# Group statistics by one sum and one sum of squares, bias on GpSimd, and a loop on TensorE, in a normalize-and-convolve kernel

## The chip, the cores and the metric

The kernel runs on one core of a Trainium2 chip. The metric is the device time of one execution in microseconds (us), the median of several runs. A core has TensorE (PE; PEld is its weight load), VectorE (DVE), ScalarE (ACT), GpSimd (POOL) and SyncE (SP), which run side by side and wait for each other by semaphores, and 16 DMA engines that move data between the memory of the chip (HBM) and the on-chip buffer SBUF. TensorE writes to PSUM.

## The reference

For 8 images of 32 channels and 128 x 128 points, fp32:

```python
def _gn(v, G=16, eps=1e-5):            # groups of 2 channels
    g = v.reshape(B_, G, C_ // G, H_, W_)
    m = jnp.mean(g, axis=(2, 3, 4), keepdims=True)
    s = jnp.var(g, axis=(2, 3, 4), keepdims=True)
    return ((g - m) / jnp.sqrt(s + eps)).reshape(v.shape)

# _L0_conv_ref: zero-padded to 256 x 256, fft2 of x and of the 3x3 weights (norm="ortho"),
# product summed over input channels, ifft2, real part, and then a window of it:
    sh = (fft_H - out_h) // 2          # 64
    out = sp[:, :, sh:sh + out_h, sw:sw + out_w]
    return out + bias[None, :, None, None]

x = x + _L0_conv_ref(_gn(x), weight, bias, 1, 1)
```

The window starts 64 rows and columns into the padded result. So the convolution reaches only one corner of the output (66 x 66 points, 33 x 33 of each parity), scaled by 1/256; everywhere else the output is x plus the bias. The statistics still need every point of x.

## The kernel before

The host lays x out so that a partition holds one of the four (row, column) parities of a channel: 4 x 32 = 128 partitions of 64 x 64 points for an image, two images to a pair. The loads are cut as below and are all issued at once on SyncE:

```python
for img in range(2):                       # images 0 and 1: two halves each
    for half in range(2):
        load(xts[img][:, rows, :], x[0, :, img, rows, :])
        if img == 0 and half == 0:
            weights_in = load(wb_sb, wb)
for img in range(2):                       # images 2 and 3: one load each
    loaded[2 + img] = [(H, load(xts[2 + img], x[1, :, img]))]
for pair in range(2, NPAIR):               # images 4 to 7: one load a pair
    loaded[2 * pair] = loaded[2 * pair + 1] = [(H, load(pairs[pair], x[pair]))]
```

Every instruction is recorded by a helper, `put(engine, emit, *needs)`, that gives it the waits it needs. The steps of an image:

```python
def take_stats(img):                       # VectorE: 8 x BN_STATS of 512 elements
    for s in range(NSTAT):
        put("dve", lambda e: e.bn_stats(stats[img][:, s, :], ...), *rows_in(...))
def aggregate(img):                        # VectorE aggregate; ScalarE: the terms to be averaged
    mv_ok = put("dve", lambda e: e.bn_aggr(mv, ...))
    put("act", lambda e: e.activation(t[:, 0:NSIGN], signs, AF.Identity, scale=mv[:, 0:1]), mv_ok, bias_ok)
    put("act", lambda e: e.activation(t[:, NSIGN:], mv[:, 1:2], AF.Identity, bias=eps, scale=float(FFT * FFT)))
def group(img):                            # TensorE: average over the 8 partitions of a group
    put("pe", lambda e: e.matmul(ps_ms[:, 0 : NSIGN + 1], avg, terms[img], start=True, stop=True), ...)
def normalize(img):
    square_ok = put("act", ... activation(squares, ps_ms[:, 1:NSIGN], AF.Square, accum_out=var[:, 0:1]) ...)
    copied = put("dve", ... tensor_copy(var[:, 1:2], ps_ms[:, NSIGN : NSIGN + 1]) ...)
    std_ok = put("act", ... activation(std, var[:, 0:1], AF.Sqrt, bias=var[:, 1:2]) ...)
    rstd_ok = put("dve", ... reciprocal(rstd[:, 0:1], std) ...)
    shift_ok = put("act", ... activation(rstd[:, 1:2], ps_ms[:, 0:1], AF.Identity, scale=rstd[:, 0:1]) ...)
    for rows in (slice(0, ROWS + 1), slice(ROWS + 1, N)):        # g in two pieces, 12 and 21 rows
        normal[img].append(put("act", lambda e: e.activation(g[:, rows, :], xt[...], AF.Identity,
                           bias=rstd[:, 1:2], scale=rstd[:, 0:1]), shift_ok, ...))
def add_bias(img):                         # ScalarE: x + bias where the convolution doesn't reach
    for part in (low, right):              # 1984 and 1023 elements a partition
        put("act", lambda e: e.activation(part, part, AF.Identity, bias=bias_sb), *free)
def multiply(img, n):                      # TensorE: 4 matmuls for a third of the image
    for k in range(4):
        put("pe", lambda e: e.matmul(ps[...], w_sb[:, k * P : (k + 1) * P], g[...],
            start=(k == 0), stop=(k == 3)), w_ok, normal[img][min(n, 1)], ...)
def add(img, first, last):                 # VectorE: x + convolution + bias
    put("dve", lambda e: e.scalar_tensor_tensor(part, in0=ps, scalar=bias_sb, in1=part, ...), *conv_ok[img], bias_ok)
```

An fp32 matmul shows in the profile as two matmuls and two weight loads. The order:

```python
keep_warm(H // 2, 2); take_stats(0); aggregate(0); group(0); warm_ok = keep_warm(0, 1)
normalize(0); add_bias(0); take_stats(1)
for img in range(B):
    more = img + 1 < B
    multiply(img, 0); multiply(img, 1)
    if more: aggregate(img + 1)
    if img:
        add(img - 1, 0, NCHUNK)
        ...                                # stores: pairs 0 and 1 whole, then images 4, 5, 6
    if more:
        group(img + 1); normalize(img + 1); add_bias(img + 1)
    multiply(img, 2)
    if img + 2 < B: take_stats(img + 2)
store(low rows of image 7); add(7, 0, 2); add(7, 2, NCHUNK); store(the rest of image 7)
```

Before that, VectorE builds `avg` (ones over 8 within a group, else zero) from what GpSimd has made, and ScalarE spreads bias, signs and weights to the four parities in 20 small copies (`spread`). TensorE's instructions are written out, all 107 matmuls.

Of the kernel before, what the change touches and what calls it, by code (L numbers as in the profile page):

```python
# [30 lines left out]
STATS = 8  # L32
BANK = 512
NSIGN = 8
# [3 lines left out]
class Queues:  # L38
# [5 lines left out]
    def __init__(self, nc):  # L44
        self.nc = nc
        self.names = {"pe": nc.tensor, "dve": nc.vector, "act": nc.scalar, "pool": nc.gpsimd, "sp": nc.sync}
        self.sems = {}
        self.done = {}
        self.seen = {name: {} for name in self.names}
        for name in self.names:  # L50
            if name != "sp":
                self.sems[name] = nc.alloc_semaphore(f"done_{name}")
                self.done[name] = 0
# [9 lines left out]
    def __call__(self, name, emit, *needs, mark=False, adds=None):  # L63

        engine, seen = self.names[name], self.seen[name]
        waits = {}
        for token, of in needs:
            if seen.get(of, 0) < token[of]:
                waits[of] = max(waits.get(of, 0), token[of])
        for token, of in needs:  # L70
            self._learn(name, token)
        waits = list(waits.items())
        for of, value in waits[:-1]:
            engine.wait_ge(self.sems[of], value)
        op = emit(engine)
        if waits:
            of, value = waits[-1]
            op.wait_op(self.sems[of], value, "sem-ge")
        if adds is not None:
            of, by = adds, LANDED  # L80
        elif mark:
            of, by = name, 1
        else:
            return None
        op.then_inc(self.sems[of], by)
        self.done[of] += by
        return {**seen, of: self.done[of]}, of


def conv_preact_kernel(nc: bass.Bass, x: bass.AP, wb: bass.AP, out: bass.AP):  # L90
# [7 lines left out]
    NSTAT = H // STATS  # L98
# [9 lines left out]

    pairs = [sbuf(f"x{pair}", P, 2, H, W) for pair in range(NPAIR)]
    xts = [pairs[img // 2][:, img % 2] for img in range(B)]  # L110
    wb_sb = sbuf("wb_sb", C, 9 * C + 4 * (1 + NSIGN))
# [7 lines left out]
    for img in range(2):  # L119
        loaded[img] = []  # L120
        for half in range(2):
            rows = slice(half * H // 2, (half + 1) * H // 2)
            loaded[img].append((rows.stop, load(xts[img][:, rows, :], x[0, :, img, rows, :])))
            if img == 0 and half == 0:
                weights_in = load(wb_sb, wb)
# [9 lines left out]

    pair = sbuf("pair", P, P // 2, 2)
# [4 lines left out]
    pair_ok = put("pool", lambda e: e.memset(pair, 0.125), mark=True)  # L141
    for step, base in ((-1, 0), (1, 1)):
# [8 lines left out]
    w_zero = put("pool", lambda e: e.memset(w_sb, 0.0), mark=True)  # L151
    eps_ok = put("dve", lambda e: e.memset(eps, EPS * FFT * FFT), mark=True)
    pair2 = pair.rearrange("p a b -> p (a b)")
    sums = put(
        "dve", lambda e: e.tensor_add(avg[:, 0 : 2 * C], pair2[:, 0 : 2 * C], pair2[:, 2 * C : 4 * C]),
# [3 lines left out]
        "dve", lambda e: e.tensor_add(avg[:, 2 * C : 3 * C], avg[:, 0:C], avg[:, C : 2 * C]), sums, mark=True  # L159
    )  # L160
    for k in (0, 1, 3):
        avg_ok = put(
            "dve", lambda e: e.tensor_copy(avg[:, k * C : (k + 1) * C], avg[:, 2 * C : 3 * C]), sums, mark=True
        )

    put("act", lambda e: e.activation(warm, eps, AF.Sqrt), eps_ok)  # L166

    bs_sb = sbuf("bs_sb", P, 1 + NSIGN)  # L170
    bias_sb, signs = bs_sb[:, 0:1], bs_sb[:, 1:]
    taps = wb_sb[:, 0 : 9 * C].rearrange("p (a b o) -> p a b o", a=3, b=3)
    w6 = w_sb.rearrange("p (dr dc r q o) -> p dr dc r q o", dr=2, dc=2, r=2, q=2)
    places = {

        0: ((0, slice(0, 1), slice(2, 3)), (1, slice(0, 2), slice(0, 2))),
        1: ((0, slice(0, 2), slice(1, 3)), (1, slice(1, 2), slice(0, 1))),
    }

    def spread(to, of):  # L180
        return put("act", lambda e: e.activation(to, of, AF.Identity), weights_in, w_zero, mark=True)  # L181

    for q in range(4):
        rin, cin = q // 2, q % 2
        to = slice(q * C, (q + 1) * C)
        of = 9 * C + q * (1 + NSIGN)
        bias_ok = spread(bs_sb[to, :], wb_sb[:, of : of + 1 + NSIGN])
        for dr, r, a in places[rin]:
            for dc, c, b in places[cin]:
                w_ok = spread(w6[to, dr, dc, r, c, :], taps[:, a, b, :])  # L190

    gs = [sbuf(f"g{k}", P, N, N) for k in range(2)]
    stats = [sbuf(f"stats{img}", P, NSTAT, 6) for img in range(B)]
    mvs = [sbuf(f"mv{k}", P, 2) for k in range(B)]
    terms = [sbuf(f"terms{k}", P, NSIGN + 1) for k in range(B)]
    squares = [sbuf(f"square{k}", P, NSIGN - 1) for k in range(B)]
    variances = [sbuf(f"var{k}", P, 2) for k in range(B)]
    stds = [sbuf(f"std{k}", P, 1) for k in range(B)]
    rstds = [sbuf(f"rstd{k}", P, 2) for k in range(B)]
# [3 lines left out]
    stats_ok, terms_ok, group_ok, means_read, normal, conv_ok, biased, added = {}, {}, {}, {}, {}, {}, {}, {}  # L203
    warm_ok = None

    def take_stats(img):
        for s in range(NSTAT):
            stats_ok[img] = put(
                "dve",
                lambda e: e.bn_stats(  # L210
                    stats[img][:, s, :],
                    xts[img][:, STATS * s : STATS * (s + 1), :].rearrange("p h w -> p (h w)"),
                ),
                *rows_in(img, STATS * (s + 1)), mark=s == NSTAT - 1,
            )

    def aggregate(img):

        mv, t = mvs[img], terms[img]
        mv_ok = put(  # L220
            "dve", lambda e: e.bn_aggr(mv, stats[img].rearrange("p n s -> p (n s)")), stats_ok[img], mark=True  # L221
        )
        put("act", lambda e: e.activation(t[:, 0:NSIGN], signs, AF.Identity, scale=mv[:, 0:1]), mv_ok, bias_ok)  # L223
        terms_ok[img] = put(
            "act",
            lambda e: e.activation(t[:, NSIGN:], mv[:, 1:2], AF.Identity, bias=eps, scale=float(FFT * FFT)),  # L226
            mark=True,
        )

    def group(img):  # L230

        group_ok[img] = put(
            "pe",
            lambda e: e.matmul(ps_ms[:, 0 : NSIGN + 1], avg, terms[img], start=True, stop=True),  # L234
            terms_ok[img], avg_ok, *means_read.get(img - 1, ()), mark=True,
        )

    def normalize(img):
        xt, g, var, std, rstd = xts[img], gs[img % 2], variances[img], stds[img], rstds[img]

        square_ok = put(
            "act",
            lambda e: e.activation(squares[img], ps_ms[:, 1:NSIGN], AF.Square, accum_out=var[:, 0:1]),  # L243
            group_ok[img], mark=True,
        )
        copied = put(

            "dve", lambda e: e.tensor_copy(var[:, 1:2], ps_ms[:, NSIGN : NSIGN + 1]), square_ok, mark=True  # L248
        )

        std_ok = put(
            "act", lambda e: e.activation(std, var[:, 0:1], AF.Sqrt, bias=var[:, 1:2]), square_ok, copied, mark=True  # L252
        )
        rstd_ok = put("dve", lambda e: e.reciprocal(rstd[:, 0:1], std), std_ok, mark=True)  # L254
        shift_ok = put(
            "act",
            lambda e: e.activation(rstd[:, 1:2], ps_ms[:, 0:1], AF.Identity, scale=rstd[:, 0:1]),  # L257
            rstd_ok, mark=True,
        )
        means_read[img] = (copied, shift_ok)  # L260
        normal[img] = []
        for rows in (slice(0, ROWS + 1), slice(ROWS + 1, N)):
# [7 lines left out]
                    shift_ok, *rows_in(img, H), *conv_ok.get(img - 2, ()), mark=True,  # L270
# [3 lines left out]
    def add_bias(img):  # L274
# [4 lines left out]
        free = [*normal[img]] + ([warm_ok] if img == 0 else [])  # L279
        biased[img] = [  # L280
            put("act", lambda e: e.activation(part, part, AF.Identity, bias=bias_sb), *free, mark=True)  # L281
# [3 lines left out]
    def multiply(img, n):  # L285
# [3 lines left out]
        for k in range(4):  # L289
# [4 lines left out]
            needs = [w_ok, normal[img][min(n, 1)]] + added.get(img - 2, [])  # L294
            ok = put(
                "pe",
                lambda e: e.matmul(  # L297
# [28 lines left out]
    def keep_warm(first, times):  # L326
        piece = xts[0][:, first : first + STATS, :].rearrange("p h w -> p (h w)")
        for _ in range(times):
            ok = put(
                "pe", lambda e: e.matmul(ps_w, avg, piece, start=True, stop=True),  # L330
                avg_ok, *rows_in(0, H), mark=True,
# [3 lines left out]
    keep_warm(H // 2, 2)  # L335
    take_stats(0)
    aggregate(0)
    group(0)
    warm_ok = keep_warm(0, 1)
    normalize(0)  # L340
    add_bias(0)
    take_stats(1)
    for img in range(B):
        more = img + 1 < B
        multiply(img, 0)
        multiply(img, 1)
        if more:
            aggregate(img + 1)
        if img:
# [3 lines left out]
            elif img > 4:  # L353
                store(out[(img - 1) // 2, :, (img - 1) % 2], xts[img - 1], *finished(img - 1))
        if more:
            group(img + 1)
            normalize(img + 1)
            add_bias(img + 1)
        multiply(img, 2)
        if img + 2 < B:  # L360
            take_stats(img + 2)
# [60 lines left out]
```

## Time and profile before

| | |
|---|---|
| median of 3 runs | 84.51 us (84.22 to 84.69) |
| span of the profiled execution | 82.9 us |
| instructions in the profile | 697 |
| busy: PE, DVE, ACT, POOL | 65.0, 54.5, 52.0, 2.3 us |
| moved by DMA | 33.63 MB, mean 405 GB/s |

The profile is of one execution. Times in it are counted from the start of the span. A group of instructions is given by its line in the kernel, engine, operation, output<-input, shape, count, busy time in us and mean ns of one, and then the idle time of the engine before it. Names are the program's own without buffer numbers: `ps` is the result of the convolution, `ps_m` the averaged statistics, `g` the normalized corner. The 16 completion marks of a transfer, one from each DMA engine, and the single packets are also in the trace.

### The profile page before, as it was taken

Reading aid. Unit: us, or ns where it says so; the run is one execution under the profiler, and the core shown is the slowest. Engines: PE = TensorE matmul, PEld = TensorE weight load, DVE = VectorE, ACT = ScalarE, POOL = GpSimd, SP = SyncE. Lnnn points to the kernel's source line nnn. Section 1 sums busy time; section 2 is a strip of 40 time slices with the busy share of each in tenths; the row PEclk is TensorE's granted clock in tenths of the full one; section 3 lists DMA queues with packets and bytes.
Section 4 is the critical chain, followed back from the end, with each engine's and each line's share of the span. In section 5 each row is a group of like instructions: output and inputs, shape, how many; then the busy total and the mean of one; then the engine's idle time right before and its main releaser. Section 6 shows DMA issues by size and latency. Waiting matters only on the chain.

```text
span 82.9 us, 697 instructions
## 1 busy us (share of the span) xinstructions
PE 65.0 (78%) x214; PEld 39.4 (47%) x214; DVE 54.5 (66%) x103; ACT 52.0 (63%) x102; POOL 2.3 (3%) x8
## 2 busy tenths in 40 slices
PE   0000999999999999999999999999999999950000
PEld 0000431666666656666666665666566566610000
DVE  0329946991999699799969988996998160042000
ACT  6109527995996699489759948984995797000000
POOL 6400000000000000000000000000000000000000
PEclk9999999999999999999999999999999999998555
DMA  2899999999996997999889998998999999999991
GB/s 40 332 411 431 407 442 478 387 427 450 514 490 269 506 490 324 427 506 474 292 364 442 442 490 348 427 506 379 427 387 427 435 411 466 403 442 400 417 430 82
DMA packets 2211, 33.63 MB, mean 405 GB/s; under 512 B 256, under 2 KB 288, under 8 KB 416
## 3 DMA queue, kind: packets, MB, share of 16 engines
q1 hardware_dynamic: 2208, 33.60, 96.1%
q8 instruction: 1, 0.02, 0.1%
q14 instruction: 2, 0.02, 0.1%
HBM read 16.82 MB, written 16.78 MB: 405 GB/s over the span
## 4 chain that ended last, share of the span: by engine, by line
PE 76%; DMA 8%; DVE 2%; ACT 2%; SPq 1%; issue 1%
PE ps L297 70%; DMA x<-x_dram 8%; PE ps_w L330 5%; DVE x L312 2%; PE ps_m L234 1%; SPq L117 1%; ACT g L266 1%; ACT std L252 0%; ACT square L243 0%; ACT rstd L257 0%; DVE rstd L254 0%; DVE var L248 0%
## 5 line engine op out<-in xcount | busy, mean ns | idle before, releaser
L297 PE MATMUL ps<-g,w_sb 128*128 128x363 f32 (+1 forms) x192 | 59.0, 464 | 0.2 <-ACT g L266 0.2
L297 PEld LDWEIGHTS ps<-g,w_sb 128*128 128x128 f32 x192 | 35.2, 189 | 21.6 <-ACT g L266 2.0
L210 DVE BATCH_NORM_STATS2 stats<-x 128x6 f32<-128x512 f32 x64 | 38.7, 678 | 2.5 <-DMA x<-x_dram 2.4
L281 ACT ACTIVATE x<-x,bs_sb 128x1984 f32<-128x1984 f32 (+1 forms) x16 | 23.9, 1543 | 0.3
L312 DVE SCALAR_TENSOR_TENSOR x<-ps,bs_sb,x 128x1089 f32<-128x1089 f32 (+2 forms) x9 | 10.5, 1179 | 7.2 <-PE ps L297 7.2
L266 ACT ACTIVATE g<-x,rstd 128x396 f32<-128x396 f32 (+1 forms) x16 | 12.7, 840 | 0.3
L330 PE MATMUL ps_w<-x,avg 128*128 128x512 f32 x6 | 5.8, 1111 | 8.4 <-DMA x<-x_dram 8.4
L330 PEld LDWEIGHTS ps_w<-x,avg 128*128 128x128 f32 x6 | 1.7, 328 | 9.4 <-DMA x<-x_dram 8.4
L243 ACT ACTIVATE square<-ps_m 128x7 f32<-128x7 f32 x8 | 1.4, 178 | 5.7 <-PE ps_m L234 5.7
L248 DVE COPY var<-ps_m 128x1 f32<-128x1 f32 x8 | 1.3, 158 | 5.1 <-ACT square L243 5.1
L223 ACT ACTIVATE terms<-bs_sb,mv 128x8 f32<-128x8 f32 x8 | 2.4, 303 | 3.5 <-DVE mv L221 3.5
L234 PEld LDWEIGHTS ps_m<-terms,avg 128*128 128x128 f32 x16 | 3.2, 205 | 2.8 <-ACT terms L226 1.3
L252 ACT ACTIVATE std<-var 128x1 f32<-128x1 f32 x8 | 2.4, 297 | 1.8 <-DVE var L248 1.8
L181 ACT ACTIVATE bs_sb<-wb_sb 32x9 f32<-32x9 f32 x4 | 0.8, 212 | 3.9 <-DMA wb_sb<-wb_dram 3.8
L257 ACT ACTIVATE rstd<-ps_m,rstd 128x1 f32<-128x1 f32 x8 | 2.1, 263 | 1.8 <-DVE rstd L254 1.8
L254 DVE RECIPROCAL rstd<-std 128x1 f32<-128x1 f32 x8 | 1.3, 163 | 2.9 <-ACT std L252 2.9
L221 DVE BATCH_NORM_AGGREGATE mv<-stats 128x2 f32<-128x48 f32 x8 | 3.0, 372 | 0.3
L181 ACT ACTIVATE w_sb<-wb_sb 32x64 f32<-32x64 f32 (+2 forms) x16 | 2.8, 246 | 0.0
L234 PE MATMUL ps_m<-terms,avg 128*128 128x9 f32 x16 | 2.5, 230 | 0.0
L226 ACT ACTIVATE terms<-mv,eps 128x1 f32<-128x1 f32 x8 | 2.3, 282 | 0.0
L166 ACT ACT_TABLE_LOAD x1 | 1.3, 1283 | 0.8 <-PEq L411 0.8
L243 ACT ACTIVATION_READ_ACCUMULATOR square<-ps_m 128x1 f32 x8 | 1.6, 196 | 0.0
(12 smaller groups left out, 3.6 us busy)
## 6 DMA issues: line engine op xcount, KB each, us to landing
x<-x_dram SPq DMA_DIRECT2D x2, 4096.0 KB, 34.3
out_dram<-x SPq DMA_DIRECT2D x2, 4096.0 KB, 16.6
out_dram<-x SPq DMA_DIRECT2D x3, 2048.0 KB, 10.1
x<-x_dram SPq DMA_DIRECT2D x4, 1024.0 KB, 7.7
x<-x_dram SPq DMA_DIRECT2D x2, 2048.0 KB, 17.2
out_dram<-x SPq DMA_DIRECT2D x1, 1056.0 KB, 7.7
out_dram<-x SPq DMA_DIRECT2D x1, 992.0 KB, 11.3
wb_sb<-wb_dram SPq DMA_DIRECT2D x1, 40.5 KB, 4.8
```

What stands on the lines that cost most here:

```text
L181: return put("act", lambda e: e.activation(to, of, AF.Identity), weights_in, w_zero, mark=True)
L210: lambda e: e.bn_stats(stats[img][:, s, :], xts[img][:, STATS * s : STATS * (s + 1), :].rearrange("p h w -> p (h w)"),),
L221: "dve", lambda e: e.bn_aggr(mv, stats[img].rearrange("p n s -> p (n s)")), stats_ok[img], mark=True
L223: put("act", lambda e: e.activation(t[:, 0:NSIGN], signs, AF.Identity, scale=mv[:, 0:1]), mv_ok, bias_ok)
L234: lambda e: e.matmul(ps_ms[:, 0 : NSIGN + 1], avg, terms[img], start=True, stop=True),
L243: lambda e: e.activation(squares[img], ps_ms[:, 1:NSIGN], AF.Square, accum_out=var[:, 0:1]),
L252: "act", lambda e: e.activation(std, var[:, 0:1], AF.Sqrt, bias=var[:, 1:2]), square_ok, copied, mark=True
L266: lambda e: e.activation(g[:, rows, :], xt[:, LO + rows.start : LO + rows.stop, LO:W], AF.Identity, bias=rstd[:, 1:2], scale=rstd[:, 0:1],),
L281: put("act", lambda e: e.activation(part, part, AF.Identity, bias=bias_sb), *free, mark=True)
L297: lambda e: e.matmul(ps[:, 0:rows, 0 : N - dc], w_sb[:, k * P : (k + 1) * P], g[:, top : top + rows, dc:N], start=(k == 0), stop=(k == 3),),
L312: lambda e: e.scalar_tensor_tensor(part, in0=ps, scalar=bias_sb, in1=part, op0=ALU.add, op1=ALU.add),
L330: "pe", lambda e: e.matmul(ps_w, avg, piece, start=True, stop=True),
```

## The change

It takes the statistics in another way, moves work between the engines, and writes TensorE's part as a loop. Each image gets a *pilot*: the average of one point of each of the 8 partitions of a group, as an origin near the values, so that a sum of squares about it loses no precision. The variance is then the mean of the squares about the pilot less the square of the mean about the pilot. VectorE takes the plain sum in one instruction and ScalarE the squares in one, over the whole image. The bias of the untouched part goes from ScalarE to GpSimd, the spreading of bias and weights too, and the building of `avg` from VectorE to GpSimd. `g` is made in one piece (but for image 0). TensorE's images 0 to 5 become three rounds of a loop over two images, with the values that it waits for in registers. The aim is fewer instructions and work more evenly spread.

```diff
+    def emit_loop(self, times, steps):           # the recorded TensorE instructions as a loop
+        ...
+        # one plan of waits for all rounds: of each place the largest value, less the round's steps
+        for place in range(size):
+            waits = {}
+            for k in range(times):
+                for of, value in rounds[k][place][1]:
+                    value -= k * steps[of]
+                    if value > seen.get(of, 0):
+                        seen[of] = waits[of] = value
+            plan.append(waits)
+        ...
+        with engine.Fori(0, times):
+            for place in range(size):
+                ...
+                    engine.wait_ge(self.sems[of], values[of])
+                op = emit(engine)
 ...
+    def take_first(img, *needs):
+        first_ok[img] = put("pool", lambda e: e.tensor_copy(pilots[img % 2], xts[img][:, 0, 0:1]), ...)
+    def pilot(img):
+        pilot_ok[img] = put("pe", lambda e: e.matmul(ps_w[:, 0:1], avg, pilots[img % 2], start=True, stop=True), ...)
+    def sum_up(img):                             # two halves for image 0, else whole
+        ... put("dve", lambda e: e.tensor_reduce(sums[img % 2][:, k, 0:1], piece, AxisListType.X, ALU.add), ...)
+    def pilot_back(img):
+        origin_ok[img] = put("act", lambda e: e.activation(origins[img], ps_w[:, 0:1], AF.Identity, scale=...), ...)
+    def sum_squares(img):
+        ... put("act", lambda e: e.activation(unused[...], piece, AF.Square, bias=origins[img],
+                       accum_out=sums[img % 2][:, k, 1:2]), origin_ok[img], ...)
-    take_stats, aggregate
 ...
     def group(img):
-            lambda e: e.matmul(ps_ms[:, 0 : NSIGN + 1], avg, terms[img], start=True, stop=True),
+            lambda e, k=k: e.matmul(ps_ms[:, 0:2], avg, sums[img % 2][:, k, :], start=(k == 0), stop=(k == last)),
+    def take_std(img, between=lambda: None):
+        square_ok = put("act", ... activation(squares[img], ps_ms[:, 0:1], AF.Square, bias=origins[img]) ...)
+        var_ok = put("dve", ... tensor_scalar(variances[img], ps_ms[:, 1:2], squares[img], None, op0=ALU.subtract) ...)
+        between()                                # the pilot of image img + 1 copied back
+        std_ok = put("act", ... activation(stds[img], variances[img], AF.Sqrt, bias=eps, scale=float(FFT * FFT)) ...)
+        rstd_ok = put("dve", ... reciprocal(rstds[img][:, 0:1], stds[img]) ...)
+        shift_ok = put("dve", ... tensor_scalar(rstds[img][:, 1:2], ps_ms[:, 0:1], rstds[img][:, 0:1], -1.0, ...) ...)
     def normalize(img):
-        for rows in (slice(0, ROWS + 1), slice(ROWS + 1, N)):
+        for rows in (slice(0, ROWS + 1), slice(ROWS + 1, N)) if img == 0 else (slice(0, N),):
 ...
     def add_bias(img):
-            put("act", lambda e: e.activation(part, part, AF.Identity, bias=bias_sb), *free, mark=True)
+            put("pool", lambda e: e.tensor_scalar(part, part, bias_sb, None, op0=ALU.add), *free, mark=True)
 ...
     for img in range(B):
+        if img + 2 == B:
+            put.emit_loop(NPAIR - 1, {"act": 2 * 5, "dve": 2 * 5, "pool": 2 * 3})
         multiply(img, 0)
         multiply(img, 1)
-        if more:
-            aggregate(img + 1)
         ...                                      # add, stores: as before
+        if img + 2 < B:
+            take_first(img + 2)
+            pilot(img + 2)
         if more:
             group(img + 1)
+            take_std(img + 1, (lambda: pilot_back(img + 2)) if img + 2 < B else (lambda: None))
             normalize(img + 1)
             add_bias(img + 1)
         multiply(img, 2)
         if img + 2 < B:
-            take_stats(img + 2)
+            sum_squares(img + 2)
+            sum_up(img + 2)
```

Ahead of the loop the order is: the pilot of image 0, its sums, GpSimd's spreading of the weights (8 copies) and the bias (4), the first point of image 1, `group(0)`, `pilot(1)`, `take_std(0)`, `normalize(0)`, `add_bias(0)`, `pilot_back(1)`, and the sums of image 1.

## The prediction

> **What bounds the kernel now.** I read four views in order. First the page's slices and queues, to see which resource is never idle:
>
> ```profile
> DMA  2899999999996997999889998998999999999991
> ...
> q1 hardware_dynamic: 2208, 33.60, 96.1%
> q8 instruction: 1, 0.02, 0.1%
> q14 instruction: 2, 0.02, 0.1%
> ```
>
> The 16 DMA engines move 33.60 MB and are busy for 96.1% of the span; 16.8 MB is input, 16.8 MB output, and no compute engine gets over 78%. The two small queues carry instructions. Second, the stages at the end (columns: length, busy us of PE, PEld, DVE, ACT, POOL, clock, DMA share, GB/s):
>
> ```profile
> 78.00:80.00 2.00, 0.00 (x0) 0.00 (x0) 0.00 (x0) 0.00 (x0) 0.00 (x0) 0.50 0.99 417
> 80.00:81.00 1.00, 0.00 (x0) 0.00 (x0) 0.00 (x0) 0.00 (x0) 0.00 (x0) 0.50 0.96 406
> 81.00:82.00 1.00, 0.00 (x0) 0.00 (x0) 0.00 (x0) 0.00 (x0) 0.00 (x0) 0.50 0.28 118
> 82.00:82.90 0.90, 0.00 (x0) 0.00 (x0) 0.00 (x0) 0.00 (x0) 0.00 (x0) 0.50 0.05 19
> ```
>
> All compute is over by 75.2; transfers are full until 81, and then a few engines straggle. In the packet records 13 engines finish the last store between 80.81 and 81.50, the other three at 82.02, 82.38 and 82.55. Third, the chain that ended last, in order of time (start, length):
>
> ```profile
> 41.80 0.12 PE ps_m L234 x2
> 41.93 7.27 PE ps L297 x24
> 49.19 0.12 PE ps_m L234 x2
> ```
>
> TensorE takes 7.39 us an image without a gap. That chain is nearly a second bound, because it releases the stores. Fourth, the timeline just after the grouping matmul, the stretch that the change rewrites:
>
> ```profile
> 41.96 0.18 ACT L243 ACTIVATE square<-ps_m 128x7 f32<-128x7 f32 x1 [0.73 <-PE ps_m L234]
> 42.04 0.20 ACT L243 ACTIVATION_READ_ACCUMULATOR square<-ps_m 128x1 f32 x1
> 42.27 0.16 DVE L248 COPY var<-ps_m 128x1 f32<-128x1 f32 x1 [0.36 <-ACT square L243]
> 42.46 0.30 ACT L252 ACTIVATE std<-var 128x1 f32<-128x1 f32 x1 [0.22 <-DVE var L248]
> 42.79 0.16 DVE L254 RECIPROCAL rstd<-std 128x1 f32<-128x1 f32 x1 [0.36 <-ACT std L252]
> ...
> 42.98 0.26 ACT L257 ACTIVATE rstd<-ps_m,rstd 128x1 f32<-128x1 f32 x1 [0.23 <-DVE rstd L254]
> 43.28 1.59 ACT L266 ACTIVATE g<-x,rstd 128x396 f32<-128x396 f32 x2
> ...
> 44.12 4.51 PEld L297 LDWEIGHTS ps<-g,w_sb 128*128 128x128 f32 x16 [0.29 <-issue]
> ```
>
> The first piece of g (722 ns) is done at 44.00; TensorE, busy on the last third of the previous image, wants it at 44.12. The wait is hidden with 0.1 us to spare.
>
> **What the skill says.** "DMA: Bandwidth & Descriptors", section Queues, rings and completion order: instruction refill has its own queue row (14), and each DMA engine takes turns between rows by packets. The trace agrees: two 8 KB packets on q14 at 32.0 (0.33 and 0.41 us) and one of 16 KB on q8 at 40.4 (1.07 us), and the stragglers have fallen behind by the next landings, 41.96 to 43.69. "Runtime: NRT & Kernel Launch", section Instruction fetch mechanics: code comes in 16 KiB blocks of 256 instructions, and a branch whose target is out of the window must fetch first. The packet sizes agree; no loop is in this trace. "VectorE: DVE Perf Modes", section The perf-mode tier table: a reduction runs at one element a cycle (0.96 GHz). The trace has no reduction. "GPSIMD Engine Reference", section Engine selection: one-input operations run at roughly line rate. The trace shows it for memsets only: (525 - 205) / 384 = 0.83 ns an element.
>
> **The change, part by part.** The rows for the durations, by shape:
>
> ```profile
> L281 ACT ACTIVATE x<-x,bs_sb 128x1984 f32<-128x1984 f32 x8 | 15.6, 1951 | 0.3
> L281 ACT ACTIVATE x<-x,bs_sb 128x1023 f32<-128x1023 f32 x8 | 9.1, 1134 | 0.0
> L266 ACT ACTIVATE g<-x,rstd 128x693 f32<-128x693 f32 x8 | 7.7, 959 | 0.0
> L266 ACT ACTIVATE g<-x,rstd 128x396 f32<-128x396 f32 x8 | 5.8, 722 | 0.3
> ```
>
> *Statistics.* ScalarE loses the two bias passes (2.99 us in the timeline) and two small ones; it gains a square pass of 4096 elements, 1.951 + 2112 x 0.85 ns + the 0.2 us accumulator read = 3.9 us. With normalize (1.3) and the small ones it has about 6.2 us of work an image: under 7.39. VectorE loses eight BN_STATS (4.82 us together) and the 0.37 us aggregate; it gains one sum, estimated from the skill's rate at 4096 / 0.96 = 4.3 us. About 6.1 us. Neither is a bound; both finish about 1 us before the grouping matmul asks.
>
> *Bias on GpSimd.* 3007 elements an image: 2.5 us at the memset's rate, 4.7 us at 1.5 ns an element (my allowance for a loop that is not ideal). It matters because the next pilot is copied behind it on the same queue, and TensorE waits for that pilot 5.1 us into the image. Up to about 4.9 us nothing shows.
>
> *Short chain.* Count from S, where an image's first matmul starts. Sixteen of its matmuls take 5.09 us (21.94 to 27.03), the new pilot matmul 0.12, and ScalarE's square follows the grouping matmul's start by 0.16: S + 5.37. Then, hops of 0.03 us included: square 0.26 (as L257, which also reads a pointer), VectorE 0.16, square root 0.30, reciprocal 0.16, shift 0.16 on VectorE. Normalize starts at S + 6.56. So far it is 0.15 us shorter than before from the grouping matmul on. But normalize is now whole: 722 + 693 x 0.8 = 1.28 us instead of a first piece of 722. It ends at S + 7.84, and TensorE goes on at about S + 7.9. TensorE's own work is 7.5. So each image takes 7.9 instead of 7.39: 0.5 us uncovered, seven times.
>
> *Start.* Weights leave ScalarE (3.5 us, but while it waited for data). Pilot: input half at 5.76, copy, matmul (0.63 as the cold grouping one), copy back: squares start at 6.9, two halves of 2.0 and a read end at 11.1, grouping with two matmuls 11.95, small chain 1.2, normalize 13.13 to 14.7. In the loop all rounds share one list of waits, and the first matmul waits for ScalarE's eighth event, the pilot copied back for image 1, which stands behind both pieces of normalize: 14.95, against 14.62 before.
>
> *Loop.* TensorE's program shrinks from 107 matmuls to 60 written out. Fetches may vanish (up to 1.05 us: 82.55 back to 81.50), move, or stay.
>
> *Sum.* S of image 7 is 14.95 + 7 x 7.9 = 70.25 (66.28 before). The last store is issued 8.92 us after it (75.20 - 66.28): 79.17. From issue to first packet the first load takes 1.02 us (0.80 to 1.83): 80.2. Before, the first DMA engine came free for it at 78.28, the last at 80.02. So the slack is used up: the queue runs dry. The last store takes 80.81 - 78.28 = 2.5 us on one engine, with up to 0.8 us spread at the start (first packets at 1.83 to 2.65): 82.7 to 83.5, middle 83.1, plus 0.35 to the end of the span: 83.4, or 0.5 more than 82.9. The stragglers cost nothing more, they are ready by then. 84.51 + 0.5 = 85.0.
>
> **Rivals.** (1) Transfers stay the whole bound: the chain is covered and the loop takes the fetches away; then 83.5 to 84.5. For it: DMA is full from 2 to 81 us. Against it: the margin under normalize is 0.1 us and the change adds 0.56 to that piece. (2) GpSimd becomes the bound: at 2.2 ns an element the bias takes 6.6 us, TensorE waits 1.7 us each image, and the time goes over 90. For it: an affine select of 128 elements takes 706 ns. Against it: memset at 0.83 ns. (3) The loop stalls TensorE at its two branches back for a fetch; a microsecond or two each, 86 to 88. Against it: the loop is some 125 instructions.
>
> **Range and chances.** A tenth of a microsecond in the period is worth 0.7 us at the end once the queue is dry; I trust it to 0.15, so 84 to 86 from that alone, stretched for the rivals: 83.8 to 86.9. Over 2% faster means under 82.8, less than the stragglers could ever give: 0.02. Over 2% slower means over 86.2, a period from 8.07 or rival 2 or 3: 0.2. Between: 0.78.
>
> **What would show it.** Right: gaps of about 0.4 us on TensorE waiting for g on ScalarE at each image, starts 7.9 apart; DMA share under 0.9 somewhere from 65 on; last store issued near 79. Wrong: starts 7.4 to 7.5 apart, or pilot waits on GpSimd, or LDWEIGHTS waiting with nothing named at the loop's branch. If the last store is issued before 77 the queue stays full and only instruction packets count.

## The result and the profile after

The changed kernel takes 112.02 us (median of 6 runs, 111.66 to 114.03) against 84.25 us for the kernel before on the same chip: ratio 1.327, 95% interval 1.3225 to 1.3315. The span of the profiled execution is 110.0 us against 82.9. The prediction was 85.0, with a range to 86.9. Some executions of a kernel fall into a slower group; ratios here are of the others alone, medians and ranges of all.

The page of the changed kernel, its slices and queues (40 slices of 2.75 us, each digit a busy share in tenths):

```profile
POOL 6384007992499519980999069933996199889910
...
DMA  3999999999999990498800000898469104969986
...
q1 hardware_dynamic: 2240, 33.60, 72.8%
q14 instruction: 1, 0.01, 0.0%
```

The same 33.60 MB move, but the DMA engines are busy for 72.8% of the span instead of 96.1%; there are whole slices in which nothing moves. The transfers are no longer the bound. GpSimd, at 2.3 us of work before, is now busy for 72.6. The waits of the engines (engine, line, what it waited for, total us, times, longest) say who waits for it:

```profile
PE ps_w L253 <- POOL pilot L247: 22.1, 7, 6.0
```

One of the seven waits, the longest, is image 0's at the start; the other six make 16.1 us. The kernel before has no such wait. The chain that ended last shows one such period in order of time (start, length); the steps from 37.66 to 39.25 are the stretch after the grouping matmul, of which the prediction showed the older form:

```profile
28.97 8.13 POOL x L355 x2
37.10 0.14 POOL pilot L247
...
37.28 0.38 PE ps_w L253 x2
37.66 0.24 PE ps_m L301 x2
...
39.25 1.32 ACT g L340
...
40.73 8.12 POOL x L355 x2
```

Read it as a ring. GpSimd's two bias passes of image n (L355) take 8.13 us. Only then does its queue come to the pilot copy of image n + 2 (L247), though the data for that copy landed long ago (here image 3, at 24.29). The pilot matmul on TensorE waits for the copy, the grouping matmul of image n + 1 stands behind the pilot matmul on TensorE's queue, the small chain and g follow, and the bias of image n + 1 waits for g. One turn is 40.73 - 28.97 = 11.76 us: 8.13 of bias and 3.6 of everything else, one after the other. Before, an image took 7.39.

That adds up. The first matmul of image 0 starts at 17.13 (14.62 before). Six turns of 11.76 and a last one of 9.0, in which there is no further pilot to wait for, bring image 7's first matmul to 96.73; before, seven images of 7.38 on average brought it to 66.28. That is 30.4 us later, and the last store is issued 30.4 later as well (105.62 against 75.20). TensorE's clock has little part in it: in the last turn the granted clock was 0.50 from 85.80 to 89.20, and that turn took about 1 us more than the last turn of the run without the bias passes below (8.0); in the turns before, TensorE is in the ring with only 0.62 us (37.28 to 37.90 above). The span is 27.1 longer and not 30.4, because the stores have no queue ahead of them at the end:

```profile
106.00:108.00 2.00, 0.00 (x0) 0.00 (x0) 0.00 (x0) 0.00 (x0) 0.00 (x0) 0.57 0.81 334
108.00:109.00 1.00, 0.00 (x0) 0.00 (x0) 0.00 (x0) 0.00 (x0) 0.00 (x0) 0.50 1.00 414
```

(the stages at the end, columns as in the prediction: the DMA share comes before the GB/s). The last store has landed 4.35 us after its issue (its last mark is at 109.97), 7.67 us before (82.87): that is the difference of 3.3. The 16 KB instruction packet that fell at 40.4 before comes after the span here.

The large groups by shape (count, busy us, mean ns):

```profile
L355 POOL TENSOR_SCALAR x<-x,bias_sb 128x1984 f32<-128x1984 f32 x8 | 42.2, 5281 | 26.8 <-ACT g L340 21.9 <-ACT origin L276 4.9
L355 POOL TENSOR_SCALAR x<-x,bias_sb 128x1023 f32<-128x1023 f32 x8 | 22.9, 2858 | 0.0
L268 DVE TENSOR_REDUCE sums<-x 128x1 f32<-128x4096 f32 x7 | 30.9, 4409 | 0.0
L287 ACT ACTIVATE unused<-x,origin 128x4096 f32<-128x4096 f32 x7 | 25.9, 3698 | 0.1
```

The statistics cost what was expected (4.4 and 3.7 us). The bias costs 5281 + 2858 ns = 8.14 us an image, 2.7 ns an element.

### The profile page after: what moved, and what is told of

Its sections match the earlier page's. It is cut to its first block, busy times and chain, and to the rows that moved or that the text cites. A ratio compares the mean times of both kernels' runs of the same rounds, so it can differ in the third digit from the quotient of the medians.

```text
span 110.0 us, 695 instructions
## 1 busy us (share of the span) xinstructions
PE 75.6 (69%) x232; PEld 45.4 (41%) x232; DVE 50.1 (45%) x42; ACT 47.4 (43%) x53; POOL 72.6 (66%) x51
## 3 DMA queue, kind: packets, MB, share of 16 engines
q1 hardware_dynamic: 2240, 33.60, 72.8%
## 4 chain that ended last, share of the span: by engine, by line
POOL 45%; PE 22%; ACT 12%; DMA 7%; DVE 5%; issue 2%; SPq 1%; POOLq 0%
POOL x L355 44%; PE ps L371 15%; ACT g L340 9%; DMA x<-x_dram 7%; PE ps_w L404 3%; PE ps_w L253 2%; PE ps_m L301 2%; ACT std L320 2%; ACT square L308 2%; DVE rstd L326 1%; DVE var L313 1%; DVE x L386 1%; DVE rstd L323 1%; SPq L175 1%; POOL pilot L247 1%
## 5 line engine op out<-in xcount | busy, mean ns | idle before, releaser
L355 POOL TENSOR_SCALAR x<-x,bias_sb 128x1984 f32<-128x1984 f32 (+1 forms) x16 | 65.0, 4069 | 26.8 <-ACT g L340 21.9
L371 PE MATMUL ps<-g,w_sb 128*128 128x363 f32 (+1 forms) x192 | 66.6, 505 | 3.2 <-ACT origin L276 1.9
L371 PEld LDWEIGHTS ps<-g,w_sb 128*128 128x128 f32 x192 | 39.0, 208 | 26.8 <-issue 6.6
L268 DVE TENSOR_REDUCE sums<-x 128x1 f32<-128x4096 f32 (+1 forms) x9 | 35.4, 3937 | 7.3 <-DMA x<-x_dram 7.3
L287 ACT ACTIVATE unused<-x,origin 128x4096 f32<-128x4096 f32 (+1 forms) x9 | 29.9, 3321 | 0.8 <-DMA x<-x_dram 0.7
L253 PE MATMUL ps_w<-pilot,avg 128*128 128x1 f32 x16 | 3.2, 267 | 22.1 <-POOL pilot L247 22.1
L386 DVE SCALAR_TENSOR_TENSOR x<-ps,bias_sb,x 128x1089 f32<-128x1089 f32 (+2 forms) x9 | 10.9, 1220 | 7.5 <-PE ps L371 7.5
L340 ACT ACTIVATE g<-x,rstd 128x1089 f32<-128x1089 f32 (+2 forms) x9 | 10.7, 1202 | 3.9 <-DVE rstd L326 3.9
L247 POOL COPY pilot<-x 128x1 f32<-128x1 f32 x8 | 1.5, 184 | 4.4 <-DMA x<-x_dram 4.4
L301 PEld LDWEIGHTS ps_m<-sums,avg 128*128 128x128 f32 x18 | 3.3, 224 | 1.2 <-issue 1.0
L301 PE MATMUL ps_m<-sums,avg 128*128 128x2 f32 x18 | 3.3, 261 | 0.0
## 6 DMA issues: line engine op xcount, KB each, us to landing
out_dram<-x SPq DMA_DIRECT2D x2, 4096.0 KB, 11.1
```

The source lines that it names most:

```text
L253: "pe", lambda e: e.matmul(ps_w[:, 0:1], avg, pilots[img % 2], start=True, stop=True),
L268: lambda e: e.tensor_reduce(sums[img % 2][:, k, 0:1], piece, mybir.AxisListType.X, ALU.add),
L287: lambda e: e.activation(unused[:, rows.start * W : rows.stop * W], piece, AF.Square, bias=origins[img], accum_out=sums[img % 2][:, k, 1:2],),
L301: lambda e, k=k: e.matmul(ps_ms[:, 0:2], avg, sums[img % 2][:, k, :], start=(k == 0), stop=(k == last)),
L340: lambda e: e.activation(g[:, rows, :], xt[:, LO + rows.start : LO + rows.stop, LO:W], AF.Identity, bias=rstd[:, 1:2], scale=rstd[:, 0:1],),
L355: put("pool", lambda e: e.tensor_scalar(part, part, bias_sb, None, op0=ALU.add), *free, mark=True)
```

## Experiments

The theory after the profile: the change loses its time in that ring, and the ring has two halves, each of which is needed: the pilot copy stands behind the bias pass in GpSimd's order, and the pass itself is slow. Rivals: the TensorE loop costs the time (a fetch or register waits at each round); GpSimd's rate alone would cost it in any order; the rest of the change (the statistics, the whole normalize, the late start) has a large share.

**Order alone.** The copy of the first point is recorded ahead of the bias pass; nothing else changes.

```diff
+    take_first(2)
     add_bias(0)
 ...
-            take_first(img + 2)
             pilot(img + 2)
             ...
             normalize(img + 1)
+            if img + 3 < B:
+                take_first(img + 3)
             add_bias(img + 1)
```

> The change, with the copy of the next pilot placed ahead of the bias passes in GpSimd's queue instead of behind them. Queue theory: TensorE waits for the pilot only because its copy stands behind 8.1 us of bias; with the copy first, the chain of an image no longer holds the bias, the waits of TensorE for the pilot go (22.1 us to under 2), and GpSimd itself becomes the bound at about 8.4 us an image: eight images from about 19.5 (it now waits for image 2 first) end near 87, the last store near 91, so 91 to 94 us. If the loop on TensorE or the new statistics made the time, it stays near 112. If GpSimd's rate alone made it, whatever the order, it stays near 112 too.

Measured: 91.22 us (before in the same session: 84.28). The wait for pilots is that of the first image alone:

```profile
PE ps_w L253 <- POOL pilot L247: 6.1, 1, 6.1
```

So the order alone takes back 20.8 of the 27.8 us (in one run), with every pass as slow as it was. GpSimd is now busy for 81% of the span, with passes back to back: eight turns of some 8.2 us are the next bound.

**Without the passes.** Both bias passes work on one element, so the bias is left out of the untouched part.

```diff
-        low = xt[:, N:H, :].rearrange("p h w -> p (h w)")
-        right = xt[:, 0:N, N:W]
+        low = xt[:, N:N + 1, 0:1].rearrange("p h w -> p (h w)")
+        right = xt[:, 0:1, N:N + 1]
```

> The change with the bias passes cut to one element a partition each (leaves out the bias on nearly the whole part that the convolution doesn't reach). Queue theory: an image then takes what the last two images of the changed kernel show without a pilot to wait for, about 8.2 us (5.2 to the grouping matmul, 3.05 from there to the next image); from 17.1 seven of these give 74.5, plus 8.9 to the last store, plus about 4: span 87 to 88, time 87.5 to 90. My prediction's own period of 7.9 from 14.95 would give 85. If the loop stalls TensorE, over 95.

Measured: 90.17 us (88.94 to 91.01), ratio 1.0726 (1.0659 to 1.0793). The chain of this kernel:

```profile
16.68 5.08 PE ps L371 x16
...
23.46 1.31 ACT g L340
...
24.82 5.08 PE ps L371 x16
```

With GpSimd out of the way an image takes 24.82 - 16.68 = 8.14 us, because TensorE waits until g is made. That is the mechanism the prediction named, 0.24 us larger than it put it. It and the start, 2.06 us later than before, are what is left of the slowdown, about 6 us.

**GpSimd's rate alone.** The kernel before, with the bias passes moved to GpSimd in the form of the change.

```diff
-            put("act", lambda e: e.activation(part, part, AF.Identity, bias=bias_sb), *free, mark=True)
+            put("pool", lambda e: e.tensor_scalar(part, part, bias_sb, None, op0=ALU.add), *free, bias_ok, mark=True)
```

> The kernel before with one thing changed: the bias of the untouched part by GpSimd instead of ScalarE. Nothing on TensorE's path waits for GpSimd here. Theory that GpSimd's rate is a bound of its own: eight images of 8.13 us plus a gap of 0.1 from 15.5 end at 81.3; the last store can't go before, and lands 4.3 us later: span about 86, time 87 to 88. Rival, that the bias is harmless when it is off TensorE's chain: within 1 us of 84.3. If GpSimd's passes slowed VectorE at the shared buffer, the BN_STATS would take more than 678 ns and the images more than 7.4 us.

Measured: 85.74 us, ratio 1.0165 (1.0125 to 1.0206). The chain ends in one piece:

```profile
15.54 64.89 POOL x L281 x16
```

Sixteen passes without a gap. The same 65 us of GpSimd work that stand behind 112 us cost 1.5 us where nothing on another engine waits behind them. I had expected 87 to 88, with gaps between the images that were not there. So the slow pass alone is not the cause: something on TensorE's path has to wait behind it.

**Without the loop.** The changed kernel, with TensorE's instructions written out.

> The change with TensorE's instructions written out again instead of the loop. Queue theory: the same within 1.5 us as with the loop, 110.5 to 112.5, the first matmuls about 1 us sooner since they no longer wait for the pilot of image 1; instruction packets come back in the middle of the span. If the loop cost the time, it falls to about 90.

Its edit: the list `put.kept` isn't started and `emit_loop` isn't called. Measured: 111.62 us in one run, span 110.2. The loop's part in the slowdown is at most a few tenths. Two things differ in the trace: image 0 starts at 15.97 instead of 17.13, since it no longer waits for the pilot of image 1, which gains nothing because the ring sets the pace; and two 16 KB instruction packets are back in the span (at 56.4 and 98.1 us).

**The loop alone.** The kernel before, with the loop of the change over TensorE's images 0 to 5.

```diff
-    terms = [sbuf(f"terms{k}", P, NSIGN + 1) for k in range(B)]
+    terms = [sbuf(f"terms{k}", P, NSIGN + 1) for k in range(2)]
 ...
+    put.kept = []
     for img in range(B):
+        if img + 2 == B:
+            put.emit_loop(NPAIR - 1, {"act": 2 * 8, "dve": 2 * 5})
```

> The kernel before with one thing changed: TensorE's images 0 to 5 as three rounds of a loop over two images (the averaged terms then lie in two buffers in turn). If an instruction fetch on one DMA engine is what makes it a straggler, the 16 KB packet at 40.4 us leaves the span, and the last store's landing marks move closer (before: 80.8 to 82.5): 83.4 to 84.2 us, 0.1 to 0.9 under the kernel before. If the loop has a cost of its own in branches or waits on registers, TensorE shows gaps at every second image and the time is over 84.5.

Measured: 84.56 us, ratio 1.0028 (1.001 to 1.0047). A miss: no gain, and a loss of a quarter of a per cent. The 16 KB packet did not leave the span, it moved from 40.4 to 71.55 us, nearer to the end, and five of the last store's 16 marks come after 82.1, up to 83.05, where it was three, up to 82.87.

**Which operations are slow on GpSimd.** On the version with the pilot first, the 1984-element pass of images 1 to 6 is replaced by other operations of the same size (so the result of the untouched part isn't x + bias).

```diff
+        forms = {
+            1: lambda e: e.tensor_scalar(low, low, 0.5, None, op0=ALU.add),
+            2: lambda e: e.tensor_copy(low, low),
+            3: lambda e: e.tensor_tensor(low, low, low, op=ALU.add),
+            4: lambda e: e.memset(low, 0.5),
+            5: lambda e: e.tensor_scalar(xt[:, N:H, :], xt[:, N:H, :], bias_sb, None, op0=ALU.add),
+            6: lambda e: e.tensor_scalar(low, low, 0.5, 2.0, op0=ALU.add, op1=ALU.mult),
+        }
```

> The rate of GpSimd by itself: the variant with the pilot copied first, where the pass over the 1984 low elements is another operation in each image (image 1: an immediate added instead of the bias; 2: a copy; 3: x + x from two inputs; 4: a memset; 5: the bias over the same elements as 31 rows of 64; 6: two immediates; 0 and 7: the bias). This replaces the bias by other things, so the output isn't the reference's. If the per-partition operand is what makes 2.66 ns an element, images 1 and 6 take under 2.2 us and image 2 too; if it is the arithmetic of this engine, 1 and 6 take about 5.3 us and only the memset 1.7 us.

The groups of this kernel (mean ns of one after the busy us):

```profile
L362 POOL TENSOR_SCALAR x<-x,bias_sb 128x1984 f32<-128x1984 f32 x2 | 10.6, 5294 | 3.3 <-ACT g L340 3.3
...
L355 POOL TENSOR_SCALAR x<-x 128x1984 f32<-128x1984 f32 x1 | 5.2, 5213 | 0.0
L357 POOL TENSOR_TENSOR x<-x 128x1984 f32<-128x1984 f32 x1 | 3.5, 3495 | 1.9 <-ACT g L340 1.9
L360 POOL TENSOR_SCALAR x<-x 128x1984 f32<-128x1984 f32 x1 | 1.9, 1853 | 0.0
L356 POOL COPY x<-x 128x1984 f32<-128x1984 f32 x1 | 1.8, 1842 | 0.0
```

The memset takes 1766 ns, and the bias add written over rows 5291. So the pass is not slow because of its operand: adding a constant takes 5213 ns. What is slow is the one-operation form of `tensor_scalar`. With a second operation, add and then multiply, the same instruction takes 1853 ns, the time of a copy, and less than an add of two whole inputs (3495).

**The two-operation form, on the changed kernel.** Add the bias, then multiply by one.

```diff
-            put("pool", lambda e: e.tensor_scalar(part, part, bias_sb, None, op0=ALU.add), *free, mark=True)
+            put("pool", lambda e: e.tensor_scalar(part, part, bias_sb, 1.0, op0=ALU.add, op1=ALU.mult), *free, mark=True)
```

> The change with one thing edited: the bias on GpSimd is written with two operations, add the bias and then multiply by 1.0, instead of the add alone. In the run on rates the form with two operations took 1.85 us for 1984 elements, the add alone 5.2 to 5.3. If the missing second operation is what is slow, whatever the operand, both passes take 1.85 + 1.0 = 2.9 us, the pilot is there in time, and the kernel behaves like the one without bias: 8.14 us an image, 88.5 to 90.5 us. If the per-partition operand is slow as well, the passes stay near 8 us and the time near 112.

Measured: 90.09 us (89.05 to 90.87; before 84.34), as expected. Its groups:

```profile
L355 POOL TENSOR_SCALAR x<-x,bias_sb 128x1984 f32<-128x1984 f32 x8 | 15.4, 1925 | 39.7 <-ACT g L340 34.8 <-ACT origin L276 4.9
L355 POOL TENSOR_SCALAR x<-x,bias_sb 128x1023 f32<-128x1023 f32 x8 | 9.1, 1138 | 0.0
```

The pilot copy still stands behind the bias, but 3.06 us of bias are over before TensorE asks. This edit of one line takes back about 22 us, as much as leaving the bias out, and an image takes the same 8.13 us. With the order alone this shows both halves of the ring: either one broken is enough.

**A first mending, with VectorE.** The pilot first, g in two pieces for every image, the smaller bias pass on VectorE (which the changed kernel leaves some time free), the larger one on GpSimd in the slow form.

```diff
+    take_first(2)
-    add_bias(0)
+    add_bias(0, "pool")
 ...                                            # and after the sums of image 1
+    add_bias(0, "dve")
```

> The change with its costs mended: the pilot copied first, GpSimd keeps the 1984 low elements (5.28 us an image, no longer a bound), VectorE takes the 1023 right ones, and g is made in two pieces again. From the run without bias (8.14 us an image) less 0.58 us for the first piece of g: 7.55 to 7.7 an image; first matmul of image 7 at 16.7 + 7 x 7.6 = 69.9, last store 8.9 later, landing 4 later: span 82.9 to 83.5, time 84.3 to 85.5. If the statistics path has another cost that the bias has hidden, images stay above 8 us. If VectorE and GpSimd get in each other's way, the right pass takes well over 0.8 us.

Measured: 101.02 us, ratio 1.1949 (1.1897 to 1.2002). A miss by 16 us. I then made the load of weights and bias one piece a partition (2304 bytes, padded on the host) instead of two of 772 (GpSimd's memset of the gap between them goes with it):

```diff
-                weights_in = load(wb_sb[:, :, 0 : 6 * C + 1], wb)
+                weights_in = load(wb_sb, wb)
```

> The same as the mended variant, with weights and bias as one run of 2304 bytes a partition (the gap is sent as zeros) instead of two of 772. In every run with the two runs the second half of image 0 has landed at 9.1 to 9.6 us instead of 8.4 before. If the form of that load is the cause, it lands at 8.4 to 8.7 again and everything of the start moves up by 0.7 us, worth up to 0.7 us in the time; if GpSimd's or another engine's early work is the cause, it stays at 9.1 or later.

Measured: 100.34 us, ratio 1.1916 (1.1849 to 1.1983). The second half of image 0 is now there (all its marks) at 8.63 us, against 9.39 in the version before this one, 9.55 in the changed kernel and 8.36 in the kernel before. In all seven versions with two pieces it is there at 9.10 to 9.55, in the three with one piece of 2304 bytes at 8.57 to 8.63. The form is not all that moves it: in the kernel before with the loop, whose load is one piece too, one mark came at 9.03. But the loss is elsewhere, and its timeline shows where:

```profile
24.73 5.27 POOL L353 TENSOR_SCALAR x<-x,bias_sb 128x1984 f32<-128x1984 f32 x1
27.15 3.42 DVE L353 TENSOR_SCALAR x<-x,bias_sb 128x1023 f32<-128x1023 f32 x1
```

VectorE's pass ends at 30.57, 0.57 us after GpSimd's. Six of the eight passes took 3.37 to 3.42 us. The other two, at 18.73 and 83.27, took 0.76 and 0.77: they began about 0.1 us before GpSimd's pass, and that pass then took 5.81 and 5.75 us instead of 5.28. The Trainium skill, "SBUF — State Buffer", section Who interferes with whom, says that a VectorE `tensor_scalar` in its two-port mode and a GpSimd instruction block each other for the whole instruction, and that the one that issues first has the way. The trace doesn't show the mode, but the times agree: above, VectorE is held until 30.00 and then works some 0.6 us; in the two other cases GpSimd is held for 0.5. VectorE's queue then carries 9.8 us an image, and that was the bound.

**All of it.** The two-operation form on GpSimd, g in two pieces, the weights in one piece, and the pilot of image 1 copied back before image 0 is normalized, with TensorE's last warm-up round after that pilot's matmul.

```diff
-    take_std(0)
+    take_std(0, lambda: pilot_back(1))
+    warm_ok = keep_warm(0, 1, w_ok, origin_ok[1])
     normalize(0)
     add_bias(0)
-    pilot_back(1)
 ...
-        for rows in (slice(0, ROWS + 1), slice(ROWS + 1, N)) if img == 0 else (slice(0, N),):
+        for rows in (slice(0, ROWS + 1), slice(ROWS + 1, N)):
```

> The change with all four costs mended: bias in the two-operation form (2.9 us on GpSimd), g in two pieces, weights in one run of 2304 bytes a partition, and the pilot of image 1 copied back ahead of normalize. By my sums: first matmul at 15.0, 7.56 us an image (8.14 less 0.58), image 7 at 67.9, last store issued at 76.8, just early enough for the queue not to run dry; and with the small programs no fetch of 16 KB falls into the span, so the last store's marks lie close together near 81.5: 83.2 to 84.0 us, up to 1 us under the kernel before. If the queue runs dry after all or the two small fetches hit one DMA engine, 84.3 to 85.3.

Measured: 84.74 us, ratio 1.0028 (1.0005 to 1.005). Its chain:

```profile
15.91 5.83 PE ps L370 x16
...
29.64 7.22 PE ps L370 x24
...
37.20 7.22 PE ps L370 x24
```

Image 0 starts at 15.91 and an image takes 7.55 us, with no wait of TensorE in between. So the statistics by sum and squares can be had at almost no loss (0.3%, just clear of the noise), and at no gain. The transfers are nearly the whole bound again: their share is 0.87 between 60 and 70 us and about 1 from there to 82. This profile is of an execution of 86.17 us; 15 of the 23 took 84.33 to 84.84 and the other eight 85.51 to 86.30.

**Without the last warm-up round.**

```diff
-    keep_warm(H // 2, 2, origin_ok[0])
+    warm_ok = keep_warm(H // 2, 2, origin_ok[0])
 ...
-    warm_ok = keep_warm(0, 1, w_ok, origin_ok[1])
```

> The mended version without the third of TensorE's warm-up rounds ahead of image 0. If the start is what still holds it back: first convolution matmul at about 15.1 us instead of 15.9, 7.56 us an image as before, the last store issued at about 77.5 instead of 78.4, and 83.6 to 84.3 us. If TensorE's granted clock falls in the gap of about 1.4 us that this leaves, or if the transfers are by now the bound, 84.5 or more.

Measured: 86.32 us, ratio 1.0265 (1.0216 to 1.0313): slower. The idle gap ahead of image 0 is 1.9 us, and the stages show the clock after it (columns as before; the clock is the number before the DMA share):

```profile
12.50:14.70 2.20, 0.37 (x4) 0.29 (x3) 1.32 (x4) 1.38 (x5) 0.00 (x0) 1.00 1.09 462
14.70:21.50 6.80, 6.72 (x18) 4.14 (x19) 3.60 (x1) 4.58 (x4) 3.16 (x3) 0.75 1.01 431
```

Image 0 starts 1.13 us earlier, at 14.78, but its 16 matmuls take 6.77 us at a clock of 0.75, against 5.83 with the round, and of the gain 0.2 is left (last store issued at 78.18 against 78.38). That explains why nothing is gained, not the loss of 1.6 us. In this profile one of the last store's 16 marks comes at 84.67, 1.28 after the one before it, and a 16 KB instruction packet held one DMA engine for 1.05 us at 73.06. The profile of the version with the round has the same: a packet of 1.04 us at 73.26, and a last mark at 84.86, 1.26 after the one before it. So the two profiles differ by no more than the 0.2 us, and the loss seems to lie in how often the late mark comes: by the times in all six runs here, in eight of 23 there (one execution of each was profiled). That the packet makes the mark late I infer from the sizes; no run shows it, and why it comes more often here is open.

**The fast form in the kernel before.** Only the two bias passes go to GpSimd, in two-operation form.

```diff
-            put("act", lambda e: e.activation(part, part, AF.Identity, bias=bias_sb), *free, mark=True)
+            put("pool", lambda e: e.tensor_scalar(part, part, bias_sb, 1.0, op0=ALU.add, op1=ALU.mult), *free, bias_ok, mark=True)
```

> The kernel before with the bias on GpSimd in the two-operation form (beside the run with the add alone, 85.7 us). GpSimd then needs 2.9 us an image instead of 8.1 and is no bound: the same as the kernel before, 84.0 to 84.6, as DMA bounds both; ScalarE is 3 us an image freer and nothing comes of it. If moving the bias costs in another way, it stays near 85.7.

Measured: 84.20 us, ratio 0.9977 (0.9959 to 0.9995), the only version under the kernel before, by a quarter of a per cent. ScalarE's work falls from 52.0 to 27.9 us, and that is worth nothing here because ScalarE was not the bound.

## Why the prediction was wrong, step by step

- **What bounds the kernel now:** right. Three divisions of the work as different as the mended change (ratio 1.0028), the kernel before with the loop (1.0028) and with its bias on GpSimd in the fast form (0.9977) lie within 0.3% of it.
- **Statistics:** right. 4.41 us on VectorE (4.3 expected), 3.70 + 0.19 on ScalarE (3.9).
- **Bias on GpSimd: the step that failed.** It put 3007 elements at "2.5 us at the memset's rate, 4.7 us at 1.5 ns an element". (The second of these should be 4.5, as 3007 x 1.5 = 4510 ns; it changes nothing.) Measured: 8.14 us. The next clause had the mechanism, that the next pilot is copied behind the bias on the same queue, and the threshold, 4.9 us. With 8.14 in its place the same working gives a wait of 3.2 us and 11.1 us an image in place of 7.9. The measured turn is 11.76 us: 8.13 of bias and 3.6 for the rest of the ring, of which the prediction had the short chain 0.24 too short. The rate came from a sentence in the Trainium skill, "GPSIMD Engine Reference", section Engine selection, that one-input operations run at roughly line rate, and from a memset, which reads nothing. For a copy (0.93 ns an element) and the two-operation form (0.93 to 0.97) that sentence holds; for the form the change uses (2.66 for the larger pass) it is off by a factor of nearly 3, and the measurement decides.
- **Rival 2** was this case: "at 2.2 ns an element the bias takes 6.6 us, TensorE waits 1.7 us each image, and the time goes over 90". It should have had far more than its part of the 0.2, since the profile of before had no row for any one-input arithmetic on GpSimd: the only arithmetic-like rows there were the affine select at 706 ns for 128 elements, which spoke for the rival.
- **Short chain:** the mechanism right, the size a bit short. Without the bias an image takes 8.14 us and not 7.9: the two small VectorE instructions that read PSUM take 0.22 us each instead of 0.16, the square starts 0.27 us after the grouping matmul instead of 0.16, and the whole g takes 1.31 us instead of 1.28.
- **Start:** the wait for the pilot of image 1 was right, its time was not: 17.13 instead of 14.95. Two things were left out. The second half of image 0 landed 1.2 us later than before (9.55); with the weights' load in one piece it landed at 8.63. And TensorE's warm-up round, which starts when that half lands (9.68) and takes 3.75 us, stands ahead of the grouping matmuls on TensorE's queue: ScalarE's squares were done at 11.67, but the grouping matmuls ended only at 14.10, where the prediction had 11.95. It had reckoned from the squares alone, though the kernel before has the same round on its chain (8.40 to 12.19).
- **Loop (rival 3):** right that it would not stall. The fetches did not vanish: in the kernel before with the loop the 16 KB packet only moved, in the changed kernel it came after the span. The prediction read the packets as agreeing with a refill row of their own (14); in the trace only the 8 KB ones are on q14, and the 16 KB one is on q8.
- **Transfers stay the whole bound (rival 1):** refuted by the DMA share of 72.8%.

The signs were well chosen: "pilot waits on GpSimd" stood among those for wrong, and that is what came.

## What to carry to other kernels

When work moves to an engine whose queue also carries a small instruction that the critical engine waits for, put the small instruction first in that queue, and work out how long the large one may take before it shows; if you don't have a measured duration of that very instruction form, give the bad case the weight of your ignorance. A change that spreads work more evenly gains nothing while the transfers are full: here the best mended version is level with the kernel before. And a one-operation `tensor_scalar` on GpSimd is worth trying in a two-operation form before the work is given to another engine.

## What the runs showed of the hardware

- GpSimd, 1984 fp32 elements a partition: add of a scalar alone 5.21 to 5.30 us, add then multiply 1.85 to 1.93, copy 1.84, memset 1.77, add of two inputs 3.50. Why the single operation is 2.8 times slower is not known.
- A VectorE `tensor_scalar` of 1023 elements takes 0.76 us when it starts just before a GpSimd pass, which then takes about 0.5 us longer, and 3.4 when it starts during one. VectorE's sums (4.41 us) took no longer beside one than before it, and GpSimd's bias took 8.12 us for image 7 too, where VectorE was idle for 6.4 of them: the slow form is not that contention.
- TensorE's granted clock was 0.75 over the 6.8 us that followed an idle gap of 1.9 us, and 16 matmuls took 6.77 us there; with a warm-up round in the gap they took 5.83, in the kernel before 5.08.
- With the load of weights and bias to 32 partitions as two runs of 772 bytes a partition instead of one of 2304, the next load landed 0.76 us later, though fewer bytes move (9.10 to 9.55 in seven versions, 8.57 to 8.63 in three).
